# A graph attention layer on one core: five shared PSUM banks, two for the scores, and a new order of loads and of the work in a step

## The chip, the core and the metric

The kernel runs on one core of one Trainium2 chip. The time is device microseconds of one execution; the figure compared is the median over several runs. PE is the matrix engine (TensorE), PEld its loading of weights, DVE the vector engine, ACT the scalar engine, POOL GpSimd, SP the queue that issues most DMAs. All arithmetic is in fp32; the products with the adjacency use fp32r.

## The reference, cut to what matters

There are 32 graphs in the batch, each of 512 nodes with 512 features, and one adjacency matrix of 512 x 512 for all. Layer 0 is masked attention with 8 heads of 64; layer 1 is a graph convolution. Each has a residual and a layer normalisation.

```python
q, k, v = (x @ Wq + bq), (x @ Wk + bk), (x @ Wv + bv)      # per head of 64
scores = einsum('bihd,bjhd->bhij', q, k) / 8 + where(adj == 0, -1e9, 0)
out = einsum('bhij,bjhd->bihd', softmax(scores), v)
x = layernorm(x + out)                                      # layer 0
y = einsum('nm,bmd->bnd', adj, x)
x = layernorm(x + (y @ weight + bias))                      # layer 1
```

## The kernel before

`fast_kernel` does the work; a second, general kernel follows it only if a check in `judge` finds sums that aren't finite or an adjacency that fp32r can't hold, and it is not run on these inputs.

The order of all engines' instructions is the order of the calls in the source (a manual schedule)[...]. So the place of a call decides what stands behind what on every engine.

**The units of work.** For a graph `b`:

- `x_transpose(b, c)` (line 253, "flips"): four transposes of a block of 128 rows into a PSUM bank `pt`, copied to `xT` by ACT.
- `project_qk` (line 261) and `project_v` (line 274): four fp32 matmuls into a bank `pm`. Queries leave PSUM by ACT, keys and values by DVE. Twelve such units make `projections(b)`.
- `scores(b, hp, half)` (line 355): for a pair of heads `hp` and two blocks `j` of keys. Each block takes two matmuls into a tile `ps` of two banks, one for each head of the pair, on 64 rows of the array each; then ACT takes the exponential into `e`, DVE multiplies by the mask `edge`, and POOL adds up `es`, the denominators' parts.
- `attend(b, hp, half)` (line 371): the products of `e` with the values into the bank `po`, on 64 columns of the array for each head; after the second half ACT copies `po` to `attT`.
- `divide(b, hp)` (line 385): the column sums of `es` by matmuls with ones, `total` by ACT, a reciprocal and a product by DVE, a sum of inverses by POOL.
- `residual(b, hp)` (line 398): four transposes of `attT` and an addition into `X[b]`. After the last pair of heads it also takes the statistics of the four row blocks and calls `normalise(b)` (line 303).
- `normalise(b)`: one square root on ACT (with its own activation table), a reciprocal, and the scalings of `X[b]` (layer 0) and of `X[b-1]` (layer 1); then `high`, the fp32r part of `X[b]`, by ACT, `low`, the rest, by DVE; then the store of `out[b-1]`.
- `aggregate(b, d)` (line 325): eight fp32r matmuls with `adjT`, copied by ACT; after the last, POOL adds the bias to `X[b]`. `convolve(b, c)` (line 338): four matmuls, an addition by DVE and the statistics.

**The steps.** A batch has 8 steps (4 pairs of heads, 2 halves). Step `i` issues the scores of step `i+1`, then units up to a part of 0.4 of its share, then `attend` of its own, then `divide` (first half) or `residual` (second half) of the pair of heads before, then the rest of its share of units (lines 436 to 468). The units of a batch are the projections of the next graph, then the aggregation of the graph before mixed with the flips of the next but one, then the convolution of the graph before. The last batch has no projections left and spreads the aggregation and the convolution of the graph before over its last six steps. `residual(b-1, 3)`, with its normalisation, falls in the second step of batch `b`: in the text this is the boundary.

**PSUM.** Eight banks: `ps` two tiles of two banks, `pm` two, `pt` one, `po` one.

**Loads.** `x`, Wk and the adjacency are issued from SP; Wq, Wv, the biases and layer 1's weight from ACT's queue, ahead of ACT's first activation.

Of the kernel before, what the change touches and what calls it, by code (L numbers as in the profile page):

```python
# [28 lines left out]
FP = mybir.dt.float32  # L29
# [14 lines left out]
def load_row(nc, pool, v, name):  # L44
    t = pool.tile([P, v.shape[0]], FP, name=name)
    nc.scalar.dma_start(t, bass.AP(tensor=v.tensor, offset=v.offset, ap=[[0, P], [1, v.shape[0]]]))
    return t


def load_col(nc, pool, v, name):  # L50
    t = pool.tile([P, v.shape[0] // P], FP, name=name)
    nc.scalar.dma_start(t, v.rearrange("(c p) -> p c", p=P))
    return t
# [133 lines left out]
def fast_kernel(ctx: ExitStack, tc, verdict, x, adj, Wq, bq, Wk, bk, Wv, bv, W1, b1, out):  # L187
# [10 lines left out]
    work = ctx.enter_context(tc.tile_pool(name="work", bufs=2))  # L198
    psum = ctx.enter_context(tc.tile_pool(name="psum", bufs=2, space=bass.MemoryType.PSUM))
    ctx.enter_context(tc.manual_schedule())  # L200


    X = {}

    def load(b):
        X[b] = work.tile([P, NB, D], FP, name="xs", bufs=4)
        nc.sync.dma_start(X[b], x[b].rearrange("(c p) d -> p c d", p=P))

    load(0)
    wq = load_weight(consts, Wq, "wq", nc.scalar)  # L210
    bq_c = load_col(nc, consts, bq, "bq_c")
    bk_c = load_col(nc, consts, bk, "bk_c")
    wk = load_weight(consts, Wk, "wk", nc.sync)
    wv = load_weight(consts, Wv, "wv", nc.scalar)
    bv_r = load_row(nc, consts, bv, "bv_r")
    adj_s = work.tile([P, NB, N], FP, name="yT", bufs=1)
    nc.sync.dma_start(adj_s, adj.rearrange("(c p) m -> p c m", p=P))
    for b in range(1, min(3, B)):
        load(b)
    w1 = load_weight(consts, W1, "w1", nc.scalar)  # L220
    b1_r = load_row(nc, consts, b1, "b1_r")
# [17 lines left out]
    def adjacency(c):  # L239
        pt = psum.tile([P, NB, P], FP, name="pt", bufs=1)  # L240
        for m in range(NB):
            nc.tensor.transpose(pt[:, m, :], adj_s[:, c, m * P:(m + 1) * P], ident)
        block = adjT[:, :, c * P:(c + 1) * P]
        nc.vector.tensor_copy(block, pt)
        cut = work.tile([P, NB, P], FP, name="attT")
        nc.vector.tensor_tensor(cut, pt, block.bitcast(FP), op=ALU.not_equal)
        nc.vector.tensor_reduce(inexact[:, c:c + 1], cut, axis=AX.XY, op=ALU.add)
        nc.vector.tensor_scalar(edge[:, :, c * P:(c + 1) * P], pt, 0.0, None, op0=ALU.not_equal)
# [4 lines left out]
    def x_transpose(b, c):  # L253
        if c == 0:
            XT[b] = work.tile([P, DB, N], FP, name="xT", bufs=1)
        pt = psum.tile([P, DB, P], FP, name="pt", bufs=1)
        for d in range(DB):
# [3 lines left out]
    def project_qk(b, hp, which):  # L261
        w, bias, store, name = (wq, bq_c, QT, "qT") if which == 0 else (wk, bk_c, KT, "kT")
        if hp == 0:
            store[b] = work.tile([P, HP, N], FP, name=name)
        pm = psum.tile([P, N], FP, name="pm")
        for d in range(DB):
# [7 lines left out]
    def project_v(b, c):  # L274
        if c == 0:
            V[b] = work.tile([P, NB, D], FP, name="v")
        pm = psum.tile([P, D], FP, name="pm")
        for d in range(DB):
# [14 lines left out]

    STAT = {}

    def statistics(row, b, slot):
        if b not in STAT:
            STAT[b] = work.tile([P, 2 * NB, 2], FP, name="stat")
        st = work.tile([P, nc.vector.BN_STATS_DIM], FP, name="bnst")
        nc.vector.bn_stats(st, row)  # L300
        nc.vector.bn_aggr(STAT[b][:, slot, :], st)  # L301

    def normalise(b):
        lo = 0 if b < B else NB
        hi = 2 * NB if b > 0 else NB
        rstd = work.tile([P, 2 * NB], FP, name="rstd")
        nc.scalar.activation(rstd[:, lo:hi], STAT[b][:, lo:hi, 1], AF.Sqrt, bias=eps)  # L307
        nc.vector.reciprocal(rstd[:, lo:hi], rstd[:, lo:hi])  # L308
        for slot in range(lo, hi):
            t = X[b] if slot < NB else X[b - 1]  # L310
            row = t[:, slot % NB, :]
            nc.vector.tensor_scalar(row, row, STAT[b][:, slot, 0:1], rstd[:, slot:slot + 1],  # L312
                                    op0=ALU.subtract, op1=ALU.mult)
        if b < B:
            high = HIGH[b] = work.tile([P, NB, D], FR, name="high", bufs=1)
            low = LOW[b] = work.tile([P, NB, D], FR, name="low", bufs=1)
            nc.scalar.activation(high, X[b], AF.Copy)
            nc.vector.tensor_sub(low, X[b], high.bitcast(FP))
        if b > 0:
            nc.sync.dma_start(out[b - 1].rearrange("(c p) d -> p c d", p=P), X[b - 1])  # L320


    YT, HIGH, LOW = {}, {}, {}

    def aggregate(b, d):
        if d == 0:
            YT[b] = work.tile([P, DB, N], FP, name="yT", bufs=1)
        pm = psum.tile([P, N], FP, name="pm")
        for part in (LOW[b], HIGH[b]):
# [8 lines left out]
    def convolve(b, c):  # L338
        pm = psum.tile([P, D], FP, name="pm")
        for d in range(DB):  # L340
            nc.tensor.matmul(pm, YT[b][:, d, c * P:(c + 1) * P], w1[:, d, :],  # L341
                             start=(d == 0), stop=(d == DB - 1))
        nc.vector.tensor_add(X[b][:, c, :], pm, X[b][:, c, :])  # L343
        statistics(X[b][:, c, :], b + 1, NB + c)

# [8 lines left out]

    def scores(b, hp, half):
        for j in (2 * half, 2 * half + 1):
            ps = psum.tile([P, 2, N], FP, name="ps")
            for s in range(2):
                lanes = slice(s * HD, (s + 1) * HD)
                nc.tensor.matmul(ps[:, s, :], KT[b][lanes, hp, j * P:(j + 1) * P], QT[b][lanes, hp, :],  # L360
                                 start=True, stop=True)
            e = E[b, hp, j] = work.tile([P, 2, N], FP, name="e", bufs=6)
            nc.scalar.activation(e, ps, AF.Exp, scale=1.0 / root)  # L363
            nc.vector.tensor_mul(e, e, edge[:, j, None, :].to_broadcast([P, 2, N]))  # L364
            if j == 1:
                ES[b, hp] = work.tile([P, 2, N], FP, name="es")
                nc.gpsimd.tensor_add(ES[b, hp], E[b, hp, 0], e)  # L367
            elif j > 1:
                nc.gpsimd.tensor_add(ES[b, hp], ES[b, hp], e)  # L369

# [14 lines left out]
    def divide(b, hp):  # L385

        es = ES.pop((b, hp))
        pm = psum.tile([P, N], FP, name="pm")
        for s in range(2):
# [8 lines left out]
    def residual(b, hp):  # L398
        at = AT.pop((b, hp))
        pt = psum.tile([P, NB, P], FP, name="pt", bufs=1)  # L400
        for c in range(NB):
# [3 lines left out]
        if hp == HP - 1:  # L405
            for c in range(NB):
                statistics(X[b][:, c, :], b, c)
            normalise(b)


    def judge():
# [8 lines left out]
        nc.vector.tensor_mul(well[:, 0:1], well[:, 0:1], well[:, 2:3])  # L420
        pm = psum.tile([P, N], FP, name="pm")
        nc.tensor.matmul(pm[0:1, 0:1], well[:, 0:1], ones[:, 0:1], start=True, stop=True)
        nc.vector.tensor_scalar(verdict, pm[0:1, 0:1], P - 0.5, None, op0=ALU.is_lt)


    for unit in flips(0) + projections(0)[:2]:
        unit[0](*unit[1:])
    for c in range(NB):
        adjacency(c)
    for unit in projections(0)[2:] + flips(1):  # L430
        unit[0](*unit[1:])

    steps = [(b, hp, half) for b in range(B) for hp in range(HP) for half in range(2)]
    per_batch = 2 * HP
    scores(*steps[0])
    for i, (b, hp, half) in enumerate(steps):
        at = i % per_batch
        if at == 0:

            units = [(u, 1.0) for u in projections(b + 1)]  # L440
            gather, turn = aggregation(b - 1), flips(b + 2)
            for k in range(NB):
                units += [(u, 0.5) for u in gather[k:k + 1]] + [(u, 0.12) for u in turn[k:k + 1]]
            units += [(u, 1.0) for u in convolution(b - 1)]

            first = 0.0 if b + 1 < B else 2.0
            share = sum(w for _, w in units) / (per_batch - first)
            done = 0.0
        if at == 3 and b > 0 and b + 2 < B:
            load(b + 2)  # L450

        def work_until(part):
            nonlocal done
            while units and done < share * (at + part - first) - 0.01:
                unit, w = units.pop(0)
                unit[0](*unit[1:])
                done += w

        if i + 1 < len(steps):
            scores(*steps[i + 1])  # L460
        work_until(0.4)
        attend(b, hp, half)
        before = steps[i - 1 - half] if i - 1 - half >= 0 else None
        if before and half == 0:
            divide(*before[:2])
        if before and half == 1:
            residual(*before[:2])
        work_until(1.0)
    divide(B - 1, HP - 1)
    residual(B - 1, HP - 1)  # L470
    judge()
    for unit in aggregation(B - 1) + convolution(B - 1):
        unit[0](*unit[1:])
    normalise(B)


# [22 lines left out]
```

## Time and profile before

| | |
|---|---|
| median of 3 runs | 3467.12 us (3466.84 to 3467.51) |
| profiled execution | 3467.39 us, of which the span from the first to the last instruction 3465.3 us |
| busy share of PE, DVE, POOL, ACT | 96%, 56%, 40%, 30% |
| granted PE clock, mean | 0.992 |
| first scores | 82.41 us after the span's start |
| one middle batch | 105.67 us, PE busy 102.97 |
| last batch and what follows | 127.9 us, PE busy 84.23 |

A line of the timeline gives the start, the time, the engine, the line of the source, the operation, the tile written and the tiles read, their shapes and how many instructions were put together; a bracket at the end gives the idle time of the engine before it and what ended that. A name with L in front is a line of the kernel.

### The profile page before, as it was taken

To read this page: it belongs to the slowest core of one execution; us is meant where nothing else is said; L and a number is where in the kernel's file an instruction comes from. 1 tells how busy PE (TensorE), PEld (TensorE's weight loads), DVE (VectorE), ACT (ScalarE), POOL (GpSimd) and SP (SyncE) were. 2 spreads that over 40 slices of the span, in tenths; PEclk is the share of its full clock that TensorE was granted. 3 is DMA by queue.
4 is the path that set the end of the run, shared out by engine and by line. 5 is a ranking of instruction groups with operands and counts; after the bars stand their busy time and mean duration, and the time that the engine had idled before them with its cause. 6 is when DMAs were issued, how large, how long until landed. Compare 5 with 4: busy or idle time off the path is not lost. (4 is left out here: it accounts for less than half of the span.)

```text
span 3465.3 us, 27336 instructions
## 1 busy us (share of the span) xinstructions
PE 3310.3 (96%) x10770; PEld 1379.3 (40%) x10770; DVE 1944.2 (56%) x2137; ACT 1039.2 (30%) x1409; POOL 1395.1 (40%) x649
## 2 busy tenths in 40 slices
PE   6999999999999999999999999999999999999986
PEld 3343444443444434444434444344444344443332
DVE  2556555556645565555556455655555664555565
ACT  1332332332323323323323233333233232333331
POOL 0443434434444433344344444334443444443443
PEclk9999999999999999999999999999999999999998
DMA  3000000000000000000000000000000000000000
GB/s 115 1 0 25 25 2 23 25 25 25 25 0 25 25 25 25 11 15 25 25 25 25 1 25 25 25 25 13 13 25 25 25 25 0 25 25 25 13 12 25
DMA packets 37910, 74.69 MB, mean 22 GB/s; under 512 B 2192, under 2 KB 2192, under 8 KB 37776
## 3 DMA queue, kind: packets, MB, share of 16 engines
q1 hardware_dynamic: 34848, 69.21, 5.5%
q10 hardware_dynamic: 2928, 3.67, 0.3%
q8 instruction: 86, 1.41, 0.2%
q14 instruction: 48, 0.39, 0.0%
HBM read 39.33 MB, written 33.55 MB: 21 GB/s over the span
## 5 line engine op out<-in xcount | busy, mean ns | idle before, releaser
L369 POOL TENSOR_TENSOR es<-es,e 128x1024 f32<-128x1024 f32 x256 | 708.2, 2766 | 1268.9 <-DVE e L364 1258.9
L364 DVE TENSOR_TENSOR e<-e,edge 128x1024 f32<-128x1024 f32 x512 | 645.5, 1302 | 456.7 <-ACT e L363 456.4
L363 ACT ACTIVATE e<-ps 128x1024 f32<-128x1024 f32 x512 | 496.8, 1021 | 712.3 <-PE ps L360 711.8
L394 DVE RECIPROCAL inverse<-total 128x512 f32<-128x512 f32 x128 | 427.9, 3343 | 227.7 <-ACT total L392 227.7
L360 PE MATMUL ps<-qT,kT 64*128 64x512 f32 x2048 | 510.4, 617 | 0.3 <-ACT e L363 0.3
L267 PE MATMUL pm<-xT,wq 128*128 128x512 f32 x1024 | 470.4, 602 | 38.8 <-ACT total L392 38.1
L367 POOL TENSOR_TENSOR es<-e 128x1024 f32<-128x1024 f32 x128 | 302.4, 2363 | 508.7 <-DVE e L364 508.7
L379 PE MATMUL po<-e,v 128*64 128x512 f32 x2048 | 496.4, 605 | 0.0
L341 PE MATMUL pm<-w,yT 128*128 128x512 f32 x1024 | 466.6, 599 | 19.7 <-DVE xs L343 19.7
L267 PE MATMUL pm<-xT,wk 128*128 128x512 f32 x1024 | 473.2, 605 | 0.0
L279 PE MATMUL pm<-wv,xT 128*128 128x512 f32 x1024 | 461.6, 599 | 0.0
L396 POOL TENSOR_TENSOR inverses<-inverses,inverse 128x512 f32<-128x512 f32 x128 | 225.5, 1762 | 248.1 <-DVE inverse L394 248.1
L267 PEld LDWEIGHTS pm<-xT,wq 128*128 128x128 f32 x1024 | 188.1, 191 | 292.3 <-issue 202.6
L267 PEld LDWEIGHTS pm<-xT,wk 128*128 128x128 f32 x1024 | 184.3, 189 | 281.4 <-issue 235.6
L360 PEld LDWEIGHTS ps<-qT,kT 64*128 64x128 f32 x2048 | 176.6, 186 | 295.3 <-issue 293.6
L341 PEld LDWEIGHTS pm<-w,yT 128*128 128x128 f32 x1024 | 184.7, 190 | 257.3 <-issue 210.9
L279 PEld LDWEIGHTS pm<-wv,xT 128*128 128x128 f32 x1024 | 186.9, 190 | 249.4 <-issue 249.4
L343 DVE TENSOR_TENSOR xs<-pm,xs 128x512 f32<-128x512 f32 x128 | 88.3, 690 | 301.4 <-POOL xs L336 177.0
L379 PEld LDWEIGHTS po<-e,v 128*64 128x64 f32 x2048 | 124.4, 136 | 328.3 <-issue 301.8
L270 ACT ACTIVATE qT<-pm,bq_c 128x512 f32<-128x512 f32 x128 | 87.4, 683 | 428.7 <-PE pm L267 428.7
L383 ACT ACTIVATE attT<-po 128x512 f32<-128x512 f32 x128 | 76.4, 597 | 455.8 <-PE po L379 455.8
L281 DVE TENSOR_TENSOR v<-pm,bv_r 128x512 f32<-128x512 f32 x128 | 88.3, 690 | 208.7 <-PE pm L279 208.7
(53 smaller groups left out, 2232.0 us busy)
## 6 DMA issues: line engine op xcount, KB each, us to landing
xs<-in_x_dram SPq DMA_DIRECT2D x32, 1024.0 KB, 5.3
out_dram<-xs SPq DMA_DIRECT2D x32, 1024.0 KB, 4.3
wq<-in_L_gnn_Wq_dram ACTq DMA_DIRECT2D x1, 1024.0 KB, 9.5
wk<-in_L_gnn_Wk_dram SPq DMA_DIRECT2D x1, 1024.0 KB, 11.3
yT<-in_adj_dram SPq DMA_DIRECT2D x1, 1024.0 KB, 13.8
wv<-in_L_gnn_Wv_dram ACTq DMA_DIRECT2D x1, 1024.0 KB, 19.2
w<-in_L_gnn_weight_dram ACTq DMA_DIRECT2D x1, 1024.0 KB, 18.4
bv_r<-in_L_gnn_bv_dram ACTq DMA_DIRECT2D x1, 256.0 KB, 16.3
```

The costliest lines, as they stand in the source:

```text
L267: nc.tensor.matmul(pm, w[:, d, hp * P:(hp + 1) * P], XT[b][:, d, :], start=(d == 0), stop=(d == DB - 1))
L279: nc.tensor.matmul(pm, XT[b][:, d, c * P:(c + 1) * P], wv[:, d, :], start=(d == 0), stop=(d == DB - 1))
L281: nc.vector.tensor_add(V[b][:, c, :], pm, bv_r)
L341: nc.tensor.matmul(pm, YT[b][:, d, c * P:(c + 1) * P], w1[:, d, :], start=(d == 0), stop=(d == DB - 1))
L360: nc.tensor.matmul(ps[:, s, :], KT[b][lanes, hp, j * P:(j + 1) * P], QT[b][lanes, hp, :], start=True, stop=True)
L363: nc.scalar.activation(e, ps, AF.Exp, scale=1.0 / root)
L364: nc.vector.tensor_mul(e, e, edge[:, j, None, :].to_broadcast([P, 2, N]))
L367: nc.gpsimd.tensor_add(ES[b, hp], E[b, hp, 0], e)
L369: nc.gpsimd.tensor_add(ES[b, hp], ES[b, hp], e)
L379: nc.tensor.matmul(po[s * HD:(s + 1) * HD, :], V[b][:, j, h * HD:(h + 1) * HD], e[:, s, :], start=(j == 0), stop=(j == NB - 1))
L394: nc.vector.reciprocal(inverse, total)
L396: nc.gpsimd.tensor_add(inverses, inverses, inverse)
```

## The change

1. PSUM: one tile `ps` of two banks for scores; one pool of five banks (`bank`) for everything that used `pm` and `pt`; `po` keeps its bank.
2. Loads: all are issued from SP in the order of use, and the first `x` comes in four blocks of rows.
3. A step: the scores of one block, then `attend`, then `divide`, then the scores of the other block, then `residual`, then the units. The units' weights are changed a little.
4. `normalise(b)` becomes three functions, `normalise` for one layer, `split` for `high` and `low`, and `store`; the layer-1 normalisation and the store of graph `b-2` are called after those of layer 0 of graph `b-1`.
5. The start: eight projections stand between the four adjacency blocks.
6. The end: the last batch has no units in its steps. The aggregation of graph 30 stands between the last `divide` and the last `residual`, the convolution of graph 30 after that residual; the last convolution is normalised and stored block by block.

```diff
-    psum = ctx.enter_context(tc.tile_pool(name="psum", bufs=2, space=bass.MemoryType.PSUM))
+    psum = ctx.enter_context(tc.tile_pool(name="psum", bufs=1, space=bass.MemoryType.PSUM))
+    def bank(*shape):
+        return psum.tile([P, *shape], FP, name="bank", tag="bank", bufs=5)
...
+        if by_block:
+            for c in range(NB):
+                nc.sync.dma_start(X[b][:, c, :], x[b, c * P:(c + 1) * P, :])
...
-    load(0)
-    wq = load_weight(consts, Wq, "wq", nc.scalar)
+    load(0, by_block=True)
+    wq = load_weight(consts, Wq, "wq", nc.sync)
+    wk = load_weight(consts, Wk, "wk", nc.sync)
...
-        pm = psum.tile([P, N], FP, name="pm")
+        pm = bank(N)
...
+    def normalise(b, which, blocks=range(NB)):
+        lo, hi = blocks[0], blocks[-1] + 1
+        stat = STAT[b, which]
+        rstd = work.tile([P, NB], FP, name="rstd", bufs=4)
+        nc.scalar.activation(rstd[:, lo:hi], stat[:, lo:hi, 1], AF.Sqrt, bias=eps)
         nc.vector.reciprocal(rstd[:, lo:hi], rstd[:, lo:hi])
+        for c in blocks:
+            row = X[b][:, c, :]
+            nc.vector.tensor_scalar(row, row, stat[:, c, 0:1], rstd[:, c:c + 1],
                                     op0=ALU.subtract, op1=ALU.mult)
+    def split(b):
+        high = HIGH[b] = work.tile([P, NB, D], FR, name="high", bufs=1)
+        low = LOW[b] = work.tile([P, NB, D], FR, name="low", bufs=1)
+        nc.scalar.activation(high, X[b], AF.Copy)
+        nc.vector.tensor_sub(low, X[b], high.bitcast(FP))
+    def store(b, blocks=None):
+        for c in blocks or ():
+            nc.sync.dma_start(out[b, c * P:(c + 1) * P, :], X[b][:, c, :])
+        if blocks is None:
+            nc.sync.dma_start(out[b].rearrange("(c p) d -> p c d", p=P), X[b])
...
             for c in range(NB):
-                statistics(X[b][:, c, :], b, c)
-            normalise(b)
+                statistics(b, 0, c)
+            normalise(b, 0)
+            split(b)
...
+    first = projections(0)
+    run(flips(0) + first[:4])
     for c in range(NB):
         adjacency(c)
+        run(first[4 + 2 * c:6 + 2 * c])
+    run(flips(1))
...
+        after = steps[i + 1] if i + 1 < len(steps) else None
+        before = steps[i - 1 - half] if i - 1 - half >= 0 else None
+        if after:
+            scores(*after[:2], 2 * after[2])
         attend(b, hp, half)
         if before and half == 0:
             divide(*before[:2])
+        if after:
+            scores(*after[:2], 2 * after[2] + 1)
         if before and half == 1:
             residual(*before[:2])
+            if hp == 0 and b > 1:
+                normalise(b - 2, 1)
+                store(b - 2)
+        while units and done < share * (at + 1) - 0.01:
+            unit, w = units.pop(0)
+            run([unit])
+            done += w
+    last = B - 1
+    divide(last, HP - 1)
+    run(aggregation(last - 1))
+    residual(last, HP - 1)
+    run(convolution(last - 1))
+    if last > 0:
+        normalise(last - 1, 1)
+        store(last - 1)
     judge()
+    run(aggregation(last))
+    for c in range(NB):
+        convolve(last, c)
+        normalise(last, 1, [c])
+        store(last, [c])
```

## The prediction

> **What bounds the kernel now.** I read the page's first part, then the timeline of one middle batch, the chain of waits and the windows. The first two lines are the page's. The next two are windows: the stretch, its length, busy time of PE, PEld, DVE, ACT and POOL with their instructions, the granted PE clock, the DMA share and GB/s; one is a whole middle batch, the other the tail.
>
> ```profile
> PE 3310.3 (96%) x10770; PEld 1379.3 (40%) x10770; DVE 1944.2 (56%) x2137; ACT 1039.2 (30%) x1409; POOL 1395.1 (40%) x649
> PEclk9999999999999999999999999999999999999998
> ...
> 1015.00:1120.67 105.67, 102.97 (x339) 42.83 (x338) 60.03 (x66) 32.41 (x44) 43.52 (x20) 1.00 0.06 20
> ...
> 3337.40:3465.30 127.90, 84.23 (x291) 38.25 (x290) 83.61 (x105) 32.76 (x44) 48.97 (x24) 0.84 0.07 25
> ```
>
> PE is the bound: of a middle batch's 105.67 us it idles 2.70. The waits of PE name three stalls, 30 times each: 38.1 us for `total` (1.27 each), 23.6 for the single `pt` bank (0.79), 19.7 for `xs` at line 343 (0.66); 81.4 in all. Outside the middle PE idles 27.7 of the first 82.4 us (windows) and 43.7 of the last 127.9. PE executes the same matmuls after the change (an fp32 matmul stands in the records as two passes of 0.43 us), so the question is which idle time goes and which comes.
>
> ```profile
> 9.14 1.09 PE L258 MATMUL pt<-ident,xs 128*128 128x128 f32 x4 [9.14 <-DMA xs<-in_x_dram]
> 13.65 1.28 ACT L259 ACT_TABLE_LOAD   x1 [13.65 <-DMA bq_c<-in_L_gnn_bq_dram]
> ...
> 1037.72 0.66 PE L402 MATMUL pt<-ident,attT 128*128 128x128 f32 x4
> 1038.21 3.60 PE L267 MATMUL pm<-xT,wq 128*128 128x512 f32 x8
> 1038.41 0.69 DVE L404 TENSOR_TENSOR xs<-pt,xs 128x512 f32<-128x512 f32 x1 [1.70 <-PE pt L402]
> 1042.47 0.30 ACT L307 ACTIVATE rstd<-stat,eps 128x8 f32<-128x8 f32 x1 [2.73 <-DVE stat L301]
> 1044.99 1.91 ACT L317 ACTIVATE high<-xs 128x2048 fp32r<-128x2048 f32 x1 [2.22 <-DVE xs L312]
> 1047.50 1.28 ACT L363 ACT_TABLE_LOAD   x1
> 1048.79 1.94 ACT L363 ACTIVATE e<-ps 128x1024 f32<-128x1024 f32 x2
> 1051.36 3.70 PE L267 MATMUL pm<-xT,wq 128*128 128x512 f32 x8 [1.27 <-ACT total L392]
> ```
>
> In the first two lines ACT's queue issues loads until 13.65, so the `xT` copies and PE behind them wait. In the rest the reader sees the boundary: residual, statistics, root, `high` and the next exponentials are one chain of 10.4 us on DVE and ACT, and the two score tiles written at 1041.74 stay in PSUM till 1048.79. PE doesn't stop for that, because both `ps` buffers were filled ahead; it stops only for `total`, queued behind the exponentials.
>
> [...]
>
> ```profile
> 79.16:82.58 3.42, 2.05 (x14) 1.40 (x16) 0.00 (x0) 1.25 (x3) 0.00 (x0) 1.00 0.00 0
> 164.50:167.90 3.40, 1.80 (x12) 1.26 (x12) 0.00 (x0) 1.36 (x3) 0.00 (x0) 1.00 0.00 0
> 167.90:171.30 3.40, 3.40 (x10) 1.18 (x8) 0.04 (x1) 1.62 (x2) 0.00 (x0) 0.50 0.00 0
> ```
>
> PE was idle 1.37 us of the first window and kept its clock; it idled 1.60 of the second and ran the third at 0.50. There eight score matmuls took 3.54 us start to start (168.02 to 171.56) against 1.92 elsewhere: a lost clock costs 1.6. [...] both windows hold mostly transposes and only one lost the clock, so they count for something, but how much is open. [...]
>
> **Part by part.**
>
> *The start.* Loads leave ACT's queue; all go to SP in order of use, `x` in four blocks. Rate from the windows: 1.15 MB by 6 us, 1.95 by 8, 2.7 by 10, 3.4 by 12. `x` and Wq (2.1 MB) are in by about 9 us, Wk by 12, adj by 15, each ahead of its first use. ACT's table load is no longer late. So projections start near 9 instead of 21.0 and don't stop: 12 units of 3.43 = 41.2, 2.5 for the cold clock (two windows touched; 1.9 at 21.0), adjacency and flips 3.7: first scores at 56.4 instead of 82.41, **-26** (-23 to -28). The four extra DMA issues (0.45 each on SP) lie under the transfers. Before the steady steps, the single `ps` makes score tiles 2 and 3 wait for exponentials (1.24 each: +2.6); the flips ending batch 0 no longer share one bank (3 x 0.69 + 0.79, and the lost clock at 167.9: -4.5); if the ramp loses a clock, +0.7. Together **-1**.
>
> *The order inside a step.* Before: 8 scores, unit, products, (ones or transposes), unit. After: 4 scores, products, (ones), 4 scores, (transposes), units. Four changes of tiling mode each way, so the 102.97 us stay. I cost this at nothing; if a group of four lost its overlap, 0.23 x 16 = 3.7 a batch. Against that: at 84.67 to 86.64 a wait splits the eight in two fours, and the pair takes 1.97.
>
> *Five shared banks.* The three stalls (2.70 a batch) go: the deepest holder is a bank written five allocations earlier, long read.
>
> *One `ps` buffer.* The second scores now wait for the exponential of the first: 1.23 from their start, 1.02 the exponential, 0.06: 2.3 us, against 2.8 of cover (1.05 + 1.77, or + 1.87 without ones). It holds wherever ACT is free. At the boundary it isn't. Time from the residual's transposes (t0). PE: 0.49 to the first unit, two units 7.0, four scores 1.05, products 1.77, ones 0.96: it wants the second scores at 11.2. Chain: in the new order both exponentials and both masks stand before the residual on DVE, the second mask running 1.23 to 2.41; the residual's add begins at 2.45, not at 0.69 as before. From there 6.58 to `high` and 3.80 to the exponential (1038.41, 1044.99, 1048.79), plus 0.3 since a second root (the layer-1 normalisation, now separate) stands behind `high` on ACT, plus 1.08 for the exponential: 14.2. **A new stall of 3.0 us** where 2.70 went: +0.3 a batch, 30 batches, **+9**. Behind the waiting scores on PE stand three units; DVE's backlog (`low`, four more scalings, reciprocal) ends near 22.9, before products need it at 26.8.
>
> *The clock.* The new stall is one piece. A window loses the clock when about 1.6 us of it fall inside (2.05 if I count only the streaming of the transposes, 12 x 0.11 us). With 3.0 in a window of 3.41 at an even phase that is ((3.41-2.05)+(3.0-2.05))/3.41 = 68%, or 94% with 1.6. I take two thirds: 30 x 0.67 x 1.6 = **+31**; ends 0 [...] and +50. Not shown before, where no stall of the middle exceeds 1.3.
>
> *The end.* Before, aggregation and convolution of batch 30 filled the last batch's steps. After, these eight steps hold no unit. A pair is then a loop: products, ones, `total`, reciprocal 3.35, scaling 0.8, mask 1.2, products of the last block, scores, exponential, mask: about 14.3 us, x4 = 57, + 9 for the boundary. Then ones and aggregation 9 (cover for the reciprocal), convolution 14 (cover for the last normalisation), then DVE's four evictions, normalisation and verdict: PE idle 10; aggregation and convolution 22.9 as now. After the last matmul: 2.8 for one block, a 256 KB store instead of 1 MB, 4.8 (6.8 now). Sum 129 against 127.9; with lost clocks in the emptied steps up to 5 more: **+6** (-4 to +12).
>
> *Free edits:* waits on SP for stores move some 6 us later (`store` after the second scalings), loads keep over 5 us.
>
> **Sum.** -26 -1 +9 +31 +6 = +19 on the profiled execution's 3467.39 (span 3465.3 and 2.1 around it; the median, 3467.12, is 0.3 lower): **3486**.
>
> **Rivals.**
> 1. *The clock holds.* Same chain, no loss of clock: -26 -1 +9 +3 = -15, **3452**, faster. For it: [...] a batch (105.97) that is nearly 31 windows (105.81), so the phase could stay on the good side for many batches. Against: the window at 164.50. It decides at a clock loss under 15 / 30 = 0.5 us a batch.
> 2. *The stall is hidden too* (ACT's chain shorter than I add up): -26 -1 -81 +3 = **3362**. For it: PE at 96% has 81 us of named stalls. Against: the 10.4 us chain stands in the trace.
> 3. *Worse:* a half-idle cold window doesn't restore the clock, two are lost: +31 again, **3515**.
> 4. *The change doesn't do what it says:* if the loads were not what held the start, +26: 3512. The ACT wait on bq_c at 13.65 speaks against it.
>
> **How the numbers follow.** My case 0.52, spread 3468 to 3502; rival 1 0.27; rival 2 0.06; 3 and 4 0.10; offsets near zero 0.05. A change is told from none at 0.2%, 7 us. My case gives 0.43 slower, 0.07 same, 0.02 faster; rival 1 0.22 faster, 0.05 same; rival 2 0.06 faster; the rest 0.10 slower, 0.05 same. Slower 0.53, same 0.17, faster 0.30. The range takes in rival 1 and leaves out rivals 2, 3 and 4: 3440 to 3508.
>
> **What would show it.** First scores near 56; in each batch one PE stall of 3 us at `ps` for ACT, after the ones of the second head pair, followed by matmuls at half clock in most batches; no stall named `total` or `pt`. A batch of 105.9 with full clock means rival 1; under 104 means the chain was mis-added.

## The result, and the profile after

The changed kernel takes 3476.31 us (median of 4 runs, 3474.20 to 3485.13) against 3466.98 (4 runs, 3466.24 to 3467.51): a ratio of 1.0032 with a 95% interval of 1.0014 to 1.0050. It is **slower by 0.3%**, 9 us, by little more than can be told from no change. The forecast was 3486 us, with a chance of 0.53 for slower.

The profiled execution took 3474.26 us, its span is 3472.5. Here is where the time went, stretch by stretch (windows of both kernels; a stretch of batches runs from the first scores of one batch to those of another):

| stretch | before | after | difference | forecast |
|---|---|---|---|---|
| start to the first scores | 82.41 | 57.65 | -24.8 | -26 |
| batch 0 | 85.61 | 85.81 | +0.2 | -1 |
| batches 1 to 30 | 3169.38 | 3195.85 | +26.5 | +40 |
| last batch and what follows | 127.90 | 133.19 | +5.3 | +6 |
| span | 3465.3 | 3472.5 | +7.2 | +19 |

The first line of the changed kernel's page (busy time of each engine):

```profile
PE 3343.1 (96%) x10770; PEld 1387.1 (40%) x10770; DVE 2050.5 (59%) x2171; ACT 1069.0 (31%) x1443; POOL 1292.7 (37%) x649
```

The waits of PE, first the three that stood in the middle of the kernel before, then two of the changed kernel: engine, tile and line waiting, releaser, total us, times, longest.

```profile
PE pm L267 <- ACT total L392: 38.1, 30, 1.3
PE pt L258 <- DVE xs L404: 23.6, 30, 0.8
PE pm L341 <- DVE xs L343: 19.7, 30, 1.1
```

```profile
PE ps L371 <- ACT e L374: 94.3, 37, 8.3
...
PE bank L434 <- DVE well L432: 7.3, 1, 7.3
```

PE's busy share is still 96%, and the clock line of the page (a digit for each of 40 slices) is the same to the digit. Yet PE is busy for 32.8 us more with the same 10770 matmuls: they ran slower. The stalls named `total`, `pt` and `xs`, 81.4 us together, are gone, and a stall at `ps` in each batch has their place. The timeline of a middle boundary shows it (start, time, engine, line, operation; in brackets the idle time before and what ended it):

```profile
1442.88 0.66 PE L413 MATMUL bank<-ident,attT 128*128 128x128 f32 x4
...
1444.12 1.23 DVE L375 TENSOR_TENSOR e<-e,edge 128x1024 f32<-128x1024 f32 x1 [1.70 <-ACT e L374]
...
1445.26 0.68 DVE L415 TENSOR_TENSOR xs<-bank,xs 128x512 f32<-128x512 f32 x1
...
1449.85 1.92 DVE L319 TENSOR_SCALAR xs<-xs,stat,rstd 128x512 f32<-128x512 f32 x4
...
1451.80 1.91 ACT L325 ACTIVATE high<-xs 128x2048 fp32r<-128x2048 f32 x1 [2.20 <-DVE xs L319]
...
1453.16 1.03 PE L401 MATMUL bank<-es,ones 128*64 128x512 f32 x4
...
1454.49 1.28 ACT L374 ACT_TABLE_LOAD   x1
1455.78 1.02 ACT L374 ACTIVATE e<-ps 128x1024 f32<-128x1024 f32 x1
...
1456.86 1.13 PE L371 MATMUL ps<-qT,kT 64*128 64x512 f32 x4 [2.67 <-ACT e L374]
```

From the residual's transposes at 1442.88 the addition begins 2.38 us later (the second mask stands ahead of it), `high` 8.92, the exponential 12.90, the second scores 13.98. PE has finished the ones, and wants those scores, 1.03 after 1453.16. It idles 2.67. There are thirty such stalls: the first, where no layer-1 root stands behind `high` yet, of 2.48, the others of 2.66 to 2.67.

What one of them does to the clock is seen in windows of 3.413 us. In the clock records of both traces the granted PE clock is 1.00 or 0.50, and all its changes (9 before, 45 after) fall on one grid of 3.413 us, within 0.01; the windows are laid on that grid (stretch, length, busy time of PE, PEld, DVE, ACT and POOL, granted PE clock, DMA share, GB/s). The first three rows are one boundary, the next two another, 282 grid windows later, the last three a third.

```profile
277.94:281.35 3.41, 1.37 (x8) 0.20 (x4) 2.46 (x3) 3.38 (x5) 0.00 (x0) 1.00 0.00 0
281.35:284.76 3.41, 2.79 (x5) 1.00 (x6) 3.41 (x6) 1.81 (x4) 0.00 (x0) 0.50 0.20 74
284.76:288.18 3.42, 3.42 (x5) 1.35 (x4) 3.42 (x2) 0.36 (x1) 2.35 (x1) 0.50 0.64 237
...
1240.50:1243.91 3.41, 1.38 (x8) 0.21 (x4) 2.45 (x3) 3.38 (x5) 0.00 (x0) 1.00 0.00 0
1243.91:1247.33 3.42, 2.78 (x8) 1.17 (x9) 3.42 (x6) 2.18 (x4) 0.00 (x0) 1.00 0.18 69
1346.31:1349.72 3.41, 0.97 (x6) 0.09 (x2) 2.86 (x4) 3.38 (x5) 0.00 (x0) 1.00 0.00 0
1349.72:1353.14 3.42, 3.20 (x6) 1.18 (x7) 3.42 (x7) 1.77 (x4) 0.04 (x1) 0.50 0.30 116
1353.14:1356.55 3.41, 3.41 (x10) 1.50 (x9) 3.38 (x2) 0.00 (x0) 2.56 (x2) 1.00 0.52 191
```

A window in which PE was busy 1.37 us and idle 2.04 lost the clock for the next; one with 1.38 busy and 2.03 idle kept it. At the first boundary the rest of the stall (0.62 idle) fell into the cold window, and the clock stayed low for a second one; at the third, 0.22 idle did not hinder its return. Of the thirty stalls 16 lost a clock, 7 of them for two windows. A batch then costs 107.05 (one window) or 108.41 (two) in place of 105.40, so 9 x 1.65 + 7 x 3.01 = 35.9 us; measured over 28 batches (279.31 to 3266.34) it is 2987.0 - 28 x 105.40 = 35.8.

So batches 1 to 30, per batch: stall 2.67 in place of 2.70; PE's busy time at full clock 102.73 in place of 102.97; lost clock 1.1 to 1.2. The changed kernel's runs spread over 11 us and those of before over 1.3. The mean granted clock goes with it (0.983 in the two fastest runs, 0.982 and 0.979 in the others), which fits a loss that depends on where the windows of the grid fall; that the phase is what differs between the runs was not shown.

### The profile page after: what moved, and what is told of

Its sections match the earlier page's. It is cut to its first block, busy times and chain, and to the rows that moved or that the text cites. A ratio compares the mean times of both kernels' runs of the same rounds, so it can differ in the third digit from the quotient of the medians.

```text
span 3472.5 us, 27279 instructions
## 1 busy us (share of the span) xinstructions
PE 3343.1 (96%) x10770; PEld 1387.1 (40%) x10770; DVE 2050.5 (59%) x2171; ACT 1069.0 (31%) x1443; POOL 1292.7 (37%) x649
## 5 line engine op out<-in xcount | busy, mean ns | idle before, releaser
L375 DVE TENSOR_TENSOR e<-e,edge 128x1024 f32<-128x1024 f32 x512 | 782.3, 1529 | 683.3 <-ACT e L374 681.8
L275 PE MATMUL bank<-xT,wk 128*128 128x512 f32 x1024 | 485.4, 618 | 0.0
L275 PE MATMUL bank<-xT,wq 128*128 128x512 f32 x1024 | 466.1, 598 | 2.3 <-DMA wq<-in_L_gnn_Wq_dram 2.3
L287 PE MATMUL bank<-wv,xT 128*128 128x512 f32 x1024 | 453.2, 595 | 0.0
L353 PE MATMUL bank<-w,yT 128*128 128x512 f32 x1024 | 449.7, 592 | 0.0
L275 PEld LDWEIGHTS bank<-xT,wk 128*128 128x128 f32 x1024 | 198.0, 199 | 263.4 <-issue 263.4
L275 PEld LDWEIGHTS bank<-xT,wq 128*128 128x128 f32 x1024 | 192.5, 191 | 256.8 <-issue 255.1
L287 PEld LDWEIGHTS bank<-wv,xT 128*128 128x128 f32 x1024 | 189.5, 190 | 238.3 <-issue 238.3
L353 PEld LDWEIGHTS bank<-w,yT 128*128 128x128 f32 x1024 | 189.9, 190 | 215.4 <-issue 215.0
L308 DVE BATCH_NORM_STATS2 bnst<-xs 128x6 f32<-128x512 f32 x256 | 174.5, 682 | 5.5
```

The costliest lines, as they stand in the source:

```text
L275: nc.tensor.matmul(pm, w[:, d, hp * P:(hp + 1) * P], XT[b][:, d, :], start=(d == 0), stop=(d == DB - 1))
L287: nc.tensor.matmul(pm, XT[b][:, d, c * P:(c + 1) * P], wv[:, d, :], start=(d == 0), stop=(d == DB - 1))
L308: nc.vector.bn_stats(st, X[b][:, c, :])
```

## The experiments

Nine kernels ran. Each is the changed kernel with one edit, but for e3, which is the kernel before.

### e1: a unit ahead of the waiting scores

```diff
         if before and half == 0:
             divide(*before[:2])
+        if at == 2 and b > 0 and units:
+            unit, w = units.pop(0)
+            run([unit])
+            done += w
         if after:
             scores(*after[:2], 2 * after[2] + 1)
```

> The changed kernel with one of the three units of a batch's third step put ahead of that step's second scores, from batch 1 on. Theory (the loss is the 2.67 us wait of the second scores for the exponential behind ACT's boundary work, and the clock that this idle piece costs): the unit takes 3.6 us and covers the whole wait, no clock is lost in the middle, 3474 - 30 x 2.67 - 34 = 3360 us. Rival A (the clock is lost for another reason): only the wait goes, 3394. Rival B (the wait moves to the next bank or to the masks): 3430 or more, with a new PE wait of over 1 us a batch.

Measured: 3364.65 us (3362.02 to 3365.65), ratio to before 0.9703 [0.9687, 0.9719]. Two middle batches in one window:

```profile
1000.00:1206.00 206.00, 206.00 (x675) 85.43 (x674) 126.26 (x136) 66.68 (x90) 80.53 (x40) 1.00 0.06 21
```

PE is busy for the whole of it at full clock: no stall is left in the middle. Against the changed kernel 111.7 us went: 30 x 2.67 = 80 of stall and 36 of clock make 116, and the batch came to 102.86 instead of 102.73 (4 us over 30). One unit, moved by one place, takes away the stall and all that hangs on it.

### e2 and e5: the stall filled with idle work

Three (e2) or one (e5) extra matmuls into a spare bank before the waiting scores, their product read by nobody.

```diff
+        if at == 2 and b > 0:
+            spare = bank(N)
+            for k in range(n):                      # n = 3 in e2, 1 in e5
+                nc.tensor.matmul(spare, wq[:, k, 0:P], wk[:, k, :], start=(k == 0), stop=(k == n - 1))
         if after:
             scores(*after[:2], 2 * after[2] + 1)
```

> The changed kernel with three matmuls that nobody reads (six passes of 0.43, 2.57 us) put between the ones and the second scores of a batch's third step: the output is as before, the matmuls are additional work. The scores start no earlier, since they still wait for ACT; PE only works through the wait. Theory (idle time in one piece costs the clock): no half clock between 60 and 3340 us, 3474 - 34 = 3440. Rival A (the clock isn't lost because of the wait): the clock record stays as it is, 3474 to 3480.

> The changed kernel with one matmul that nobody reads (two passes, 0.86 us) ahead of the second scores of a batch's third step, instead of three; the output is as before. It leaves 1.81 us of the 2.67 us of idle time. Theory (a clock window of 3.41 us is lost only if 2.04 us or more of it are idle, as the 30 stalls of the changed kernel's trace say): no clock lost in the middle, the same time as with three matmuls, 3440 +- 3. Rival (the threshold lies at 1.6, as the prediction's first reading had it, or the loss grows in proportion to the idle time): 3450 to 3465.

Measured: e2 3439.82 us (3438.72 to 3441.46), 0.9923 [0.9907, 0.9940]; e5 3437.35 (3436.71 to 3437.81), 0.9916 [0.9900, 0.9933]. The scores come no earlier in either (the batch is 105.43 and 105.40, as in the changed kernel at full clock), so what fell, 36.5 and 39.0 us, is the lost clock alone. In e5 a stall of 1.61 us is left, some of it whole in one window, and no middle window lost the clock; its waits:

```profile
PE ps L371 <- ACT e L374: 61.6, 37, 7.2
```

So at this place 1.61 us of idle time in a window didn't lose the clock, and 2.04 did.

### e3: the start alone

The kernel before, with only the loads and the opening order of the change.

```diff
-    load(0)
-    wq = load_weight(consts, Wq, "wq", nc.scalar)
+    load(0, by_block=True)
+    wq = load_weight(consts, Wq, "wq", nc.sync)
...
+    first = projections(0)
+    run(flips(0) + first[:4])
     for c in range(NB):
         adjacency(c)
+        run(first[4 + 2 * c:6 + 2 * c])
+    run(flips(1))
```

> The kernel before with nothing but the change's loads (all on SP, in order of use, the first x in four blocks) and its order at the start (projections between adjacency blocks). Theory: the first scores move from 82.4 to about 58 us and nothing later changes: 3467 - 25 = 3442. Rival (the start of the changed kernel needs its five banks): with one transposing bank and two others the start stalls on adjacency and flips, 3455 or more.

Measured: 3447.66 us (3446.41 to 3448.62), 0.9945 [0.9928, 0.9962]. The first scores came at 60.11, 22.3 earlier than before and 2.5 later than in the changed kernel: with one `pt` bank each block of transposes waits for the copy of the last (0.69 to 0.75 us in its timeline). At the opening that costs nothing, since the first projection starts at 10.57 against 10.48 in the changed kernel, which waits for Wq there. It costs in the flips of graph 1, the last work ahead of the first scores, which take 4.62 here and 1.85 in the changed kernel. Their first and the first scores in e3's timeline:

```profile
55.49 0.60 PE L262 MATMUL pt<-ident,xs 128*128 128x128 f32 x4
...
60.11 1.99 PE L364 MATMUL ps<-qT,kT 64*128 64x512 f32 x8
```

The middle keeps the three stalls of before (38.0, 23.5 and 19.9 us in its waits). Loads and opening order changed together here, but the traces tell them apart. The first projection starts at 10.57 in place of 21.00: 10.4 us for the loads. The three waits for `edge` between the adjacency blocks (9.0 us before) are gone: that is the order, and with it goes the half clock behind those waits (granted 0.50 from 34.79 to 45.03), about 2.5 by my estimate: before, four transposes took 1.09 there in place of 0.63, twice, and eight matmuls 5.16 in place of 3.60. So the loads held the start, but for less than half of the gain, and about 2.5 us of the changed kernel's 24.8 belong to the shared banks. Of e3's 22.3 us, 19.3 reached the median.

### e4: two score tiles, three shared banks

```diff
-        return psum.tile([P, *shape], FP, name="bank", tag="bank", bufs=5)
+        return psum.tile([P, *shape], FP, name="bank", tag="bank", bufs=3)
...
-        ps = psum.tile([P, 2, N], FP, name="ps")
+        ps = psum.tile([P, 2, N], FP, name="ps", bufs=2)
```

> The changed kernel with two score tiles (four banks) and three shared banks in place of one and five. Theory: the scores no longer wait for ACT at the boundary, but the shared banks do: the bank of the key projection there is emptied by DVE behind the normalisations, 15.9 us after the residual's transposes, and PE wants it again at 12.3: a wait of about 3.6 us named bank for DVE in place of 2.67 for ACT, clock lost as often or more, 3474 + 28 = 3500 (3480 to 3530). Rival (three shared banks are enough): all stalls go and the clock holds, 3360.

Measured: 3373.89 us (3372.53 to 3376.00), 0.9732 [0.9716, 0.9748]. The theory fell and the rival held, 14 us above its 3360. From PE's waits:

```profile
PE ps L371 <- ACT e L374: 7.4, 2, 7.1
PE bank L343 <- ACT yT L345: 7.2, 29, 0.2
```

With a second score tile the boundary's stall is gone, and three shared banks make PE wait 0.25 us a batch. I had assumed that banks are handed out in turn, so that a projection would wait for a bank that DVE's backlog holds. At a boundary of e4 the key projection started at 1412.05 with no wait, while DVE read the previous keys from their bank only at 1414.86:

```profile
1410.67 0.67 ACT L278 ACTIVATE qT<-bank,bq_c 128x512 f32<-128x512 f32 x1
...
1412.05 3.70 PE L275 MATMUL bank<-xT,wk 128*128 128x512 f32 x8
...
1414.86 0.75 DVE L280 TENSOR_SCALAR kT<-bank,bk_c 128x512 f32<-128x512 f32 x1
```

The trace gives no bank numbers, but the bank of the ones was read only at 1413.57 (into `total`), so the one left of the three is that of the queries, which ACT had emptied at 1410.67. Together with e1 this shows two separate cures of one stall: another place for the scores, or other work ahead of them. It also shows that three shared banks are enough to keep the stalls named `total`, `pt` and `xs` away; whether the pool or the new order of a step removed them was not tried apart.

### e6: the residual ahead of the second scores

The transposes, the addition and the statistics stand ahead of the second scores; `normalise(b, 0)` and `split(b)` stand behind them, in a function `settle`.

```diff
         if before and half == 0:
             divide(*before[:2])
+        if before and half == 1:
+            residual(*before[:2])
         if after:
             scores(*after[:2], 2 * after[2] + 1)
         if before and half == 1:
-            residual(*before[:2])
+            settle(*before[:2])
```

> The changed kernel with the residual's transposes, addition and statistics ahead of a step's second scores, and the normalisation and the split behind them as now: the second mask no longer stands before the residual on DVE. Theory (the stall is the length of the chain residual, statistics, root, high, exponential): the chain starts 1.8 us earlier against PE, the stall falls from 2.67 to about 0.9, under the clock's threshold: 3474 - 53 - 34 = 3387. Rival (the wait is set by ACT's load in the step, not by where the chain starts): still about 2.7 a batch, 3470.

Measured: 3509.36 us (3506.14 to 3521.29), 1.0135 [1.0117, 1.0153]; slower than either kernel. The theory (3387) fell, and the rival's 3470 too. A middle boundary, then two clock windows of it:

```profile
1440.54 0.65 PE L413 MATMUL bank<-ident,attT 128*128 128x128 f32 x4
...
1441.23 0.69 DVE L415 TENSOR_TENSOR xs<-bank,xs 128x512 f32<-128x512 f32 x1
...
1446.48 4.01 DVE L319 TENSOR_SCALAR xs<-xs,stat,rstd 128x512 f32<-128x512 f32 x4
1446.50 2.34 POOL L378 TENSOR_TENSOR es<-e 128x1024 f32<-128x1024 f32 x1 [10.83 <-DVE rstd L316]
...
1450.53 1.91 ACT L325 ACTIVATE high<-xs 128x2048 fp32r<-128x2048 f32 x1 [4.95 <-DVE xs L319]
...
1455.59 1.13 PE L371 MATMUL ps<-qT,kT 64*128 64x512 f32 x4 [2.49 <-ACT e L374]
```

```profile
1453.68:1457.10 3.42, 1.51 (x5) 0.60 (x6) 3.38 (x7) 2.76 (x5) 0.00 (x0) 1.00 0.02 5
1457.10:1460.51 3.41, 3.41 (x5) 1.35 (x4) 3.41 (x3) 0.69 (x1) 1.78 (x1) 0.50 0.81 303
```

The addition now follows the transposes by 0.69 in place of 2.38. But the second mask now stands ahead of the reciprocal and holds it back by 0.7, and the four scalings took 4.01 us in place of 1.92, beside POOL's addition into `es` of 2.34. So `high` came 9.99 after the transposes, and the stall fell only to 2.49. The first scaling, which starts 0.02 us from POOL's addition, took 2.64 us in place of 0.55 and ended 0.28 after it, and the three behind took 0.53 each; in the changed kernel all 256 scalings took 0.54 to 0.55. What holds the scaling back was not tried by itself. The batch at full clock is also longer (106.00, PE busy 103.51, 0.78 more). This order adds one change between scores and other matmuls to each second half; at the boundary above, from the start of the products to that of the projection, with scores and transposes between, it is 3.51 us in place of 3.42. Four times 0.09 is under half of the 0.78; the rest is open. From about 1130 us on every batch of the profiled run lost a clock (mean granted clock 0.980, in the changed kernel 0.983), with a stall of 2.49 in place of 2.67. The windows say how. In every third or fourth batch the stall opens a window and score matmuls follow it, and such a window lost the clock with 1.91 us of idle time (first row; the second runs at half clock). At the changed kernel's boundaries, where products and ones fill the rest of the window, 2.03 was kept. And the first three of these batches last 324.2 us (107.64 + 109.15 + 107.43), 95 windows, so the phase recurs.

### e7, e8, e9: the end

e7 spreads the aggregation and convolution of graph 30 over the last batch's last six steps, as before the change. e8 is e1 with the verdict called later. e9 is e8 with the boundary of the last batch moved.

```diff
# e7
+            else:
+                units = [(u, 0.6) for u in aggregation(b - 1)] + [(u, 1.0) for u in convolution(b - 1)]
+            lead = 0.0 if b + 1 < B else 2.0
+            share = sum(w for _, w in units) / (per_batch - lead)
...
-    run(aggregation(last - 1))
...
-    run(convolution(last - 1))
# e8
-    judge()
     run(aggregation(last))
+    judge()
# e9
+        early = b == B - 1 and at == 1
+        if early:
+            residual(*before[:2])
         if after:
             scores(*after[:2], 2 * after[2])
```

> The changed kernel with the aggregation and the convolution of graph 30 spread over the last six steps again, as before the change, and nothing of them after the loop. Theory (emptied steps wait for the reciprocal and the masks longer than the filled end saves): the part from the last batch's start falls from 133.2 to about 127: 3468 +- 5. Rival (the filled end is the better one): 136 or more, 3478.

> The kernel with a unit ahead of the second scores of the third step, and with the verdict's matmul called after the last aggregation instead of ahead of it, so that PE does not wait for DVE's verdict first. Theory: the 7.2 us wait at the verdict and the half clock after it go, 3364.6 - 9 = 3356. Rival (the last aggregation then waits for low just as long): 3364.

> The change with a unit ahead of the waiting scores and the late verdict (the fastest kernel so far, 3355.2 us), and in the second step of the last batch alone the residual of graph 30's predecessor pair, with its normalisation, ahead of the step's first scores instead of behind its second ones. Theory: the last batch grew by the change because the residual's addition stands on DVE behind the mask of a score tile that waits for the products, which wait for two masks (after: addition at 3356.17 with the masks before it ended at 3351.35; before: addition right behind the two masks). Then the addition comes 4.8 us earlier, the stretch from the 30th `high` to the end falls from 198.7 us to 194 to 195, and the median to 3351. Rival: the first tile's exponential and mask, now behind `high` on ACT and DVE, take the gain back: the stretch stays at 198.7 within 1, the median at 3355; or it costs 2 more, 3357.

Measured: e7 3478.40 us (3473.05 to 3482.22), 1.0033 [1.0019, 1.0047], the same as the changed kernel; e8 **3355.22** (3351.98 to 3356.51), 0.9677 [0.9661, 0.9693]; e9 3355.90 (3354.93 to 3356.42), 0.9681 [0.9668, 0.9694].

e8's gain of 9.4 us over e1 comes with the wait for the verdict (7.3 us in the waits of the changed kernel), which now lies under the aggregation and is gone from the waits; e8 is the fastest version that ran, 3.2% ahead of the kernel before.

For the end itself I compare the time from the start of the 30th `high` to the end of the span, in its three parts (to the 31st `high`, to the 32nd, to the end), from the timelines:

| | to the 31st | to the 32nd | to the end | sum |
|---|---|---|---|---|
| before | 93.00 | 66.09 | 42.09 | 201.2 |
| after | 98.77 | 64.32 | 45.47 | 208.6 |
| e7 | 98.94 | 67.66 | 42.43 | 209.0 |
| e4 | 98.37 | 65.42 | 45.89 | 209.7 |
| e8 | 98.06 | 64.31 | 36.30 | 198.7 |
| e9 | 91.95 | 70.68 | 36.31 | 198.9 |

And what PE did in the whole of it, in the same columns as the clock windows: before, after, e7.

```profile
3264.12:3465.30 201.18, 155.16 (x520) 67.73 (x518) 125.88 (x146) 54.98 (x73) 82.85 (x40) 0.90 0.06 22
...
3263.94:3472.50 208.56, 165.53 (x526) 69.47 (x522) 129.79 (x153) 57.81 (x79) 78.55 (x40) 0.91 0.06 21
...
3266.97:3476.00 209.03, 159.77 (x526) 67.64 (x522) 133.88 (x153) 57.71 (x79) 79.18 (x40) 0.91 0.06 21
```

The parts of the table move work as well as time: up to the 31st `high` PE idles as long after the change as before (10.98 and 10.95 us), but 14 more matmuls now come ahead of that `high`. So the whole counts. There PE idles 3.0 less after the change and is busy 10.4 longer, with only six more matmuls. Much of that is lost clock. e7 runs the same 526 matmuls as the changed kernel and is busy 5.8 less, since its filled steps keep the clock better (0.89 of it granted between the 31st and the 32nd `high`, against 0.81). But it idles 6.2 more; its wait for the verdict is 18.1 us in place of 7.3. So the emptied steps do cost clock, about as much as the filled end saves. A second score tile (e4) doesn't help here.

e9 tried another cause. In the changed kernel's last boundary the residual's addition stands on DVE behind the mask of a score tile, and that tile's matmuls wait behind products that wait for two masks. In e9 the residual comes first, and `high` came 6.1 us earlier, with 20 fewer matmuls ahead of it; the next stretch grew by 6.4, with 20 more in it. So its first half (the place of the addition sets when `high` comes) held, and its second (that the time can be had back by this move) fell: PE had other work, and lost nothing by the later `high`. With the late verdict (e8) the whole stretch is 2.5 us shorter than before. Why e7, whose steps are filled as before the change, still needs 7.9 us more than the kernel before (3.2 of them idle) is open.

## Why the prediction was right

The direction held, and so did the mechanism: one piece of idle time of PE at each boundary, at `ps` for ACT, after the ones of the second head pair, and a loss of clock on top. 3476.3 lies in the range. By its steps:

- **The start**, -26 forecast, -24.8 measured. The projections started at 10.48, not 9, since Wq landed later than the rate of the windows gave (a wait of 2.3); the cold clock cost 2.4 (5.96 for eight matmuls against 3.60), forecast 2.5. The clock records begin only at 15.1; ahead of that the matmuls start 0.85 to 0.99 apart, as where 0.50 is granted (0.85 to 1.01 at 168.02), and soon behind it 0.43. Rival 4, that the loads were not the cause, is refuted by e3, though the opening order did as much there as the loads.
- **Batch 0**, -1 forecast, +0.2 measured.
- **The stall**, forecast 3.0, measured 2.67. The chain was 13.98 long, not 14.2: `high` came at 8.92 instead of 9.03, and the second root moved the rest by 0.2 instead of 0.3. PE's side, 11.2 forecast, was 11.3. So +9 was -1: a term of a difference of two like sizes, and a tenth of the stall is 9 us over thirty batches.
- **Work in a step at no cost**: the batch's busy time at full clock fell by 0.24, 7 us in all. I had counted equal changes of tiling mode (64*128, 128*64 and 128*128 in the lines: scores, products and the rest) and 0. That it came so near was luck: counted from start to start over one batch, the score matmuls take 16.95 us in 16 groups of four, in place of 15.34 in 8 groups of eight, so that a group of either size takes 0.20 more than its pairs of passes at 0.43 (two pairs or four); and all other matmuls, in longer runs of one kind, take 85.78 in place of 87.63.
- **The clock**, +31 forecast (its own factors, 30 x 0.67 x 1.6, give 32), about 35 measured, shown by e2 and e5. Two errors met, so the nearness is luck. Fewer windows lost the clock than two thirds (16 of 30): with the stall of 2.67 and the border at 2.04 the forecast's own formula gives 59%, or 18, so the shorter stall is most of that. But what I held a rival, two windows lost in place of one, happened in 7 of the 16, and so a loss cost 2.24 on average and not 1.6. The half-idle cold window that rival 3 spoke of wasn't half idle: 0.50 us was enough. (That rival's sum is 3517, not 3515.) Of the two readings of the border the prediction kept open, 2.05 us (counting a transpose at 0.11 us, the time from one start to the next) came near at these boundaries, where 2.03 was kept and 2.04 lost, and 1.6 didn't; but it is no rule for other work, as e6 shows, where 1.91 was lost.
- **The end**, +6 forecast, +5.3 measured. The forecast had +1 for the chain of the emptied steps and up to 5 us of lost clock. The clock is borne out by e7: the same matmuls are busy 5.8 us less with the steps filled. Idle time didn't grow: from the 30th `high` on PE idles 3.0 less than before.
- **Rivals 1 and 2.** The clock didn't hold, so 3452 fell; where it is made to hold, the kernel takes 3437 to 3440 (e5, e2). The stall was not hidden in this change, but rival 2's sum, 3362, is what the kernel gives once it is: 3364.65 in e1, 3373.89 in e4.

The sum over the span was +19 and +7 came out. The terms that missed are the stall (10 too high) and the busy time of a batch (7 too high), against 4 too low for the clock.

Two reasons of mine fell in the experiments, both about something that the profile of the kernel in hand had not shown: banks handed out in turn (e4), and a chain that starts earlier ends earlier (e6, where a scaling beside POOL's addition took 2.64 us).

## What to carry to other kernels

When several short stalls are traded for one, add up the longest piece of idle time in a clock window: here pieces of 1.61 us cost no more than themselves, and a piece of 2.67 up to 3 us more. The one score tile cost PE 2.67 us where its reader's queue was full, once a batch; so look for the longest thing that ever stands in such a queue, here a normalisation with two table loads (1.28 us each: ahead of the root and ahead of the exponential). And before restructuring, try to put one ready unit ahead of the instruction that will wait: with it the restructured kernel gained 102 us on the one before, without it it lost 9.

## What the runs showed of the hardware

Windows of 3.413 us that were far from empty lost the clock for the next, and the border was no fixed idle time: it differed with the matmuls that filled the rest of the window. At the changed kernel's boundaries, with products and ones beside the stall, 2.04 us without a matmul in a window of 3.413 lost the clock and 2.03 did not. In the last batch (3387.48 to 3390.89, the end of some scores and products) 2.01 lost it, in e6, with scores and the start of a projection, 1.91, and in the kernel before, with transposes alone (164.50 to 167.90 in the prediction), 1.60. In the other direction, a cold window with 0.22 us of idle time gave the clock back at these boundaries and one with 0.50 didn't; in the last batch one with 0.34 did (3349.93 to 3353.34). How the hardware weighs the different matmuls is open.

A scaling of 128x512 on DVE took 0.55 us alone and 2.64 in e6, beside an addition on POOL of 2.34.
